# The last twelve batches of a per-batch adapter with residual and layer norm, in a written-out order

## The chip, the cores and the metric

The kernel runs on one core of a Trainium2 chip. The metric is the device time of one execution in microseconds. TensorE does matrix products into PSUM; VectorE, ScalarE and GpSimd do elementwise work; SyncE (SP) issues nearly all transfers between the chip's memory and SBUF. Each engine takes its instructions strictly in order, and they wait for each other through semaphores.

## The reference

For each of 128 batches `b` there is an `x[b]` of 128 rows and 512 columns and a language number `id`, which picks one of ten sets of weights. All is float32.

```python
h = relu(x @ W1[id] + b1[id])            # 512 -> 128, "down"
z = x + h @ W2[id] + b2[id]              # 128 -> 512, "up"; z is a residual sum
mean, var = mean(z), mean((z - mean)**2) # over the 512 columns
out = x + (z - mean) * rsqrt(var + 1e-5) * gamma[id] + beta[id]
```

## The kernel before, in words

One batch is one tile of 128 partitions by 512 columns. `B` is 128 and `E` is `B - 5`, which is 123. Each batch passes through the same steps; the name of the helper and its line stand behind each.

- TensorE transposes `x` in four blocks (`transpose_x`, L271), ScalarE copies the result to SBUF (`copy_xT`, L275).
- ScalarE copies the batch's W1 out of a table of all ten in SBUF, at an address that depends on the identifier (`stage_w1`, L262), into a tile of a pool of seven buffers. The first seventeen batches instead load W1 by identifier from the chip's memory (`load_first`, L161).
- TensorE multiplies (`down`, L294: four products in float32, each shown as two in the profile), ScalarE applies the bias and relu (`relu`, L302), TensorE multiplies by W2 (`up`, L311), into one of five PSUM buffers called `py`. The last two batches add b2 in TensorE as well, with a product that picks a row (L310).
- GpSimd makes `r = x + b2` (`add_b2`, L281) and `o = x + beta` (`add_beta`, L288).
- VectorE adds `r` to `py` and sums the rows in the same pass (`residual`, L328); ScalarE squares the deviations and sums them (`square`, L351).
- ScalarE makes the negative mean (L342) and a first estimate of the reciprocal root (`root`, L361); VectorE improves it with one Newton step, in three small instructions (L365, L367, L370). These small ones are done for two batches at once.
- VectorE scales, `py = (py - mean) * gamma` (`scale`, L394), and finishes, `o = py * rstd + o` (`finish`, L403).
- SP stores `o` for two batches at a time (`store`, L407), 512 KB each.

The order of the work is that of the program: `keep` chains each instruction behind the one before it on its engine. The main loop (L577) runs over `i`, and a step of it holds the transposes and the down product of one batch, the up product of an earlier one, and the normalisation of still earlier ones. TensorE's order in it is: transposes of `n`, down of `n - 1`, up of `n - 2`. At the end `tail` (L463) takes over for the batches behind `E`: there batches 123, 124 and 125 leave VectorE in the last step. ScalarE makes `n` (`by_pool`, L450), GpSimd multiplies by gamma for 123 and 124 (L452) and adds `o` (L454); 126 and 127 are finished by VectorE (`finish_cols`, L461), 127 in two halves. The last stores go out by batch or half a batch, on SP and on ScalarE's queue (`store_last`, L457).

Loads of `x` come four batches at a time, 1 MB each (`load_x`, L71); the last one is for batches 124 to 127.

Of the kernel before, what the change touches and what calls it, by code (L numbers as in the profile page):

```python
# [8 lines left out]
FP = mybir.dt.float32  # L9
# [7 lines left out]
P = 128  # L17
# [5 lines left out]
U = 2  # L23
# [3 lines left out]
def cond_resid_kernel(ctx: ExitStack, tc: tile.TileContext, x, itok, W1, b1, W2, b2, gamma, beta, out):  # L27
# [286 lines left out]
    def col(tiles, b):  # L314

        return tiles[b // 2][:, b % 2 : b % 2 + 1]
# [6 lines left out]
    def residual(b):  # L323
        r = rs.pop(b) if b in rs else xb(b)
        if b % 2 == 0:
            sums[b // 2] = st.tile([P, 2], FP, tag="sum", name=f"sum_{b // 2}")
        keep(
            nc.vector.scalar_tensor_tensor(ys[b], ys[b], 1.0, r, ALU.mult, ALU.add, accum_out=col(sums, b))  # L328
        )
# [30 lines left out]
    def root(ssq, t):  # L360
        keep(nc.scalar.activation(t, ssq, AF.Abs_reciprocal_sqrt, bias=eps, scale=1.0 / H3))  # L361

    def newton(n, ssq, t, u):
        if n == 1:
            keep(nc.vector.scalar_tensor_tensor(u, ssq, EPS * H3, t, ALU.add, ALU.mult))  # L365
        else:
            keep(nc.vector.scalar_tensor_tensor(u, u, 1.0 / H3, t, ALU.mult, ALU.mult))  # L367

    def newton_3(rstd, t, u):
        keep(nc.vector.scalar_tensor_tensor(rstd, u, -3.0, t, ALU.add, ALU.mult))  # L370
# [28 lines left out]
    def finish(b):  # L399
        g, j = divmod(b, 2)  # L400
        o = os[g][:, j, :]
        keep(
            nc.vector.scalar_tensor_tensor(o, ys.pop(b), rstds[g][:, j : j + 1], o, ALU.mult, ALU.add)  # L403
        )

    def store(g):
        keep(nc.sync.dma_start(out=out[2 * g : 2 * g + 2].rearrange("b s h -> s b h"), in_=os.pop(g)))  # L407
        del rstds[g]

    def on(b):  # L410
        return 0 <= b < B
# [3 lines left out]
    shifts = {}  # L415
    halves = slice(0, H // 2), slice(H // 2, H)

    def of_one(b):
        if -b not in parts_of:
            pool, tag = {E + 3: (p_h, "h"), E + 4: (p_x, "xT")}.get(b, (p_s, "s"))  # L420
            parts_of[-b] = pool.tile([P, 1], FP, tag=tag, name=f"root_of_{b}"), st.tile([P, 1], FP, tag="part", name=f"part_of_{b}")
        return parts_of[-b]

    def rstd_of(b, n):

        t, u = of_one(b)
        if n < 3:
            newton(n, ssqs[b], t, u)
        else:
            rstds[b] = st.tile([P, 1], FP, tag="rstd", name=f"rstd_{b}")  # L430
            newton_3(rstds[b], t, u)

    def deviation_of(b):
        ssqs[b] = st.tile([P, 1], FP, tag="ssq", name=f"ssq_{b}")
        sq = tp.tile([P, H], FP, tag="sq", name=f"sq_{b}")
        keep(nc.scalar.activation(sq, ys[b], AF.Square, bias=col(sums, b), scale=-float(H), accum_out=ssqs[b]))  # L436
        root(ssqs[b], of_one(b)[0])

    def rstd_col(b):
        return rstds[b] if b > E else rstds[b // 2][:, b % 2 : b % 2 + 1]  # L440

    def shift(b):
        shifts[b] = st.tile([P, 1], FP, tag="shift", name=f"shift_{b}")
        keep(nc.vector.tensor_scalar(shifts[b], col(nmeans, b), rstd_col(b), None, ALU.mult))

    def by_pool(b, scaled, cols=slice(0, H)):

        n = rp.tile([P, H], FP, tag="r", name=f"n_{b}")[:, cols]
        bias = 0.0 if scaled else shifts[b]
        keep(nc.scalar.activation(n, ys[b][:, cols], AF.Identity, bias=bias, scale=rstd_col(b)))  # L450
        if not scaled:
            keep(nc.gpsimd.tensor_tensor(n, n, gamma_b[:, bass.ds(lid(b, ET.Pool) * H, H)], ALU.mult))  # L452
        for part in halves if b > E else (cols,):
            keep(nc.gpsimd.tensor_tensor(os[b // 2][:, b % 2, part], n[:, part], os[b // 2][:, b % 2, part], ALU.add))  # L454
# [4 lines left out]
    def finish_cols(b, cols=slice(0, H)):  # L459
        o = os[b // 2][:, b % 2, cols]  # L460
        keep(nc.vector.scalar_tensor_tensor(o, ys[b][:, cols], rstd_col(b), o, ALU.mult, ALU.add))  # L461

    def tail(b):  # L463
        p = E // 2
        residual(b)
        if b == E + 1:
            rstd(p, 1)
            scale(E - 1)
            rstd(p, 2)
            finish(E - 2)  # L470
            store(p - 1)
            rstd(p, 3)
            deviation_of(b)
            shift(E)
            by_pool(E, False)
        elif b == E + 2:
            rstd_of(b - 1, 1)
            negative_means(b // 2)
            rstd_of(b - 1, 2)
            finish_cols(E - 1)  # L480
            store_last(E - 1)
            rstd_of(b - 1, 3)
            store_last(E)
            deviation_of(b)
        elif b == E + 3:
            left, right = slice(0, H // 2), slice(H // 2, H)
            few, most = slice(0, H // 4), slice(H // 4, H)
            shift(b - 2)
            by_pool(b - 2, False)
            residual(b + 1)  # L490
            rstd_of(b - 1, 1)
            scale(b - 1)
            rstd_of(b - 1, 2)
            deviation_of(b)
            negative_means(b // 2)
            scale(b)
            rstd_of(b - 1, 3)
            rstd_of(b, 1)
            deviation_of(b + 1)
            rstd_of(b, 2)  # L500
            by_pool(b - 1, True)
            for part in halves:
                store_last(b - 2, nc.scalar, part)
            for part in halves:
                store_last(b - 1, nc.scalar, part)
            rstd_of(b, 3)
            rstd_of(b + 1, 1)
            finish_cols(b)
            store_last(b)
            rstd_of(b + 1, 2)  # L510
            scale(b + 1)
            rstd_of(b + 1, 3)
            for cols in (left, right):
                finish_cols(b + 1, cols)
                store_last(b + 1, nc.sync, cols)


    def spin(n, width):
        idle = p_s.tile([P, H], FP, tag="s", name="idle")
# [54 lines left out]
    up(1)  # L574

    turned = 5
    for i in range(3, B + U):  # L577
        b = i - U - 1
        if b > G and b % G == 2 and b // G + 3 < NG and b // G + 3 >= 5:
            load_x(b // G + 3)  # L580
        up_to = i
        if b <= E:
            if turned <= up_to and on(turned):
                transpose_x(turned)
            add_b2(b + 2)
# [18 lines left out]
        if b == E:  # L604
            add_b2(b + 3)
            add_beta(b + 1)
            add_b2(b + 4)
            for n in range(b + 2, B):
                add_beta(n)
        if b > E:  # L610
            tail(b)
        elif half == 0:
            if on(b):
                vector_b2(b)
                residual(b)
                square(b)
            if mine:
                scale(2 * p)
                rstd(p, 1)
            if old:  # L620
                finish(2 * p - 1)
                store(p - 1)
        else:
            if on(b):
                vector_b2(b)
            if mine:
                rstd(p, 2)
            if on(b):
                residual(b)
                square(b)  # L630
            if mine:
                rstd(p, 3)
                scale(2 * p + 1)
            if mine:
                finish(2 * p)
        if 0 <= g and b <= E and half == 1:
            scalar_means(g)
            deviation(g)

        for n, engine in ((turned + 2, ET.Activation), (i - U + 3, ET.PE), (b + 1, ET.DVE), (b + 6, ET.Pool)):  # L640
            if on(n):
                lid(n, engine)


# [35 lines left out]
```

## Time and profile before

| what | value |
|---|---|
| time, median of 3 runs | 304.56 us (304.44 to 304.68) |
| the profiled execution's own time | 304.08 us |
| its span, first to last instruction | 302.3 us |
| granted TensorE clock, mean | 0.993 |
| busy: TensorE, VectorE, ScalarE, GpSimd | 96%, 97%, 92%, 94% |

Four engines are busy for over nine tenths of the span, so a batch has little slack on any of them. A busy share is not the same as a bound: in the stretch where TensorE sets the pace, VectorE's share is high because its instructions overlap in the record, each starting before the record of the one before has ended. The times below are microseconds from the start of the span. The stretch that matters here is the last one, from some 277 us on:

| stretch, us | VectorE | ScalarE | GpSimd | TensorE | GB/s |
|---|---|---|---|---|---|
| 270 to 280 | 9.96 | 9.82 | 10.00 | 10.00 | 171 |
| 280 to 290 | 9.72 | 9.82 | 10.00 | 10.00 | 116 |
| 290 to 299.2 | 8.78 | 6.16 | 8.22 | 3.47 | 165 |
| 299.2 to 302.3 | 0 | 0 | 0 | 0 | 187 |

The figures are the busy microseconds of each engine in the stretch.

### The profile page before, as it was taken

The page shows a single profiled execution, that of the slowest core. Times are in us where ns is not written, and L with a number is a line of the kernel's source. Part 1 is how long each engine was busy: PE and PEld are TensorE (multiplying, and loading weights), DVE is VectorE, ACT ScalarE, POOL GpSimd, SP SyncE. Part 2 cuts the span into 40 slices and gives each one's busy share as a digit, 9 for nine tenths or more (in the row PEclk, how much of TensorE's full clock was granted, in tenths as well). Part 3 has the DMA queues.
Part 4 walks back from the last instruction along what each step waited for, and adds up shares of the span by engine and source line. Part 5 has one row for each costly group of instructions (what it writes and reads, how often), then busy time and mean ns, then how long its engine had stood idle before and what let it go on. Part 6 is the DMA issues. An engine that isn't in the chain of part 4 may idle for free.

```text
span 302.3 us, 7001 instructions
## 1 busy us (share of the span) xinstructions
PE 290.6 (96%) x1820; PEld 218.0 (72%) x1821; DVE 294.2 (97%) x784; ACT 279.6 (92%) x771; POOL 284.9 (94%) x240
## 2 busy tenths in 40 slices
PE   7899999999999999999999999999999999999980
PEld 3758787777777777777777777777777777777740
DVE  6989999999999999999999999999999999999995
ACT  5878789999999999999999999999999999999982
POOL 1299998999999999999999999999999999999995
PEclk9999999999999999999999999999999999999997
DMA  6999999986667876766678667767866666882244
GB/s 235 385 389 364 346 339 402 404 307 206 233 234 243 279 255 205 244 209 261 222 280 270 212 204 240 263 226 261 279 211 221 218 253 217 271 283 113 108 166 173
DMA packets 43929, 77.33 MB, mean 256 GB/s; under 512 B 2121, under 2 KB 8020, under 8 KB 43890
## 3 DMA queue, kind: packets, MB, share of 16 engines
q1 hardware_dynamic: 43254, 76.31, 73.5%
q10 hardware_dynamic: 636, 0.57, 0.6%
q8 instruction: 15, 0.25, 0.3%
q14 instruction: 24, 0.20, 0.2%
HBM read 43.32 MB, written 33.55 MB: 254 GB/s over the span
## 4 chain that ended last, share of the span: by engine, by line
PE 89%; DVE 5%; DMA 2%; issue 1%; ACT 1%; SPq 0%; POOL 0%; DVEq 0%; ACTq 0%; POOLq 0%
PE ph L294 36%; PE py L311 35%; PE pxT L271 18%; DMA x<-in_x_dram 2%; DVE py L394 2%; DVE py L328 1%; DVE o L403 1%; PE row L229 1%; SPq L161 0%; ACT n L450 0%; ACT sq L351 0%; ACT sq L436 0%; DVE o L461 0%; ACT w1s L262 0%; DVE rstd L370 0%
## 5 line engine op out<-in xcount | busy, mean ns | idle before, releaser
L288 POOL TENSOR_TENSOR o<-x,beta_b 128x512 f32<-128x512 f32 x128 | 170.1, 1359 | 12.7 <-DVE beta_b L247 11.6
L294 PE MATMUL ph<-xT,w1s 128*128 128x128 f32 x1024 | 135.3, 275 | 0.2 <-DMA w1s<-in_L_cond_W_dram 0.2
L281 POOL TENSOR_TENSOR r<-x,b_b 128x512 f32<-128x512 f32 x97 | 131.7, 1360 | 0.0
L311 PE MATMUL py<-w,hT 128*128 x256 | 131.3, 595 | 0.0
L294 PEld LDWEIGHTS ph<-xT,w1s 128*128 128x128 f32 x1024 | 124.8, 192 | 1.3 <-issue 0.6
L271 PEld LDWEIGHTS pxT<-ident,x 128*128 128x128 f32 x512 | 66.0, 149 | 66.8 <-issue 49.9
L394 DVE SCALAR_TENSOR_TENSOR py<-py,nmean,gamma_b 128x512 f32<-128x512 f32 x126 | 94.8, 753 | 0.0
L403 DVE SCALAR_TENSOR_TENSOR o<-py,rstd,o 128x512 f32<-128x512 f32 x122 | 91.1, 747 | 0.0
L351 ACT ACTIVATE sq<-py,sum 128x512 f32<-128x512 f32 x124 | 85.8, 692 | 0.6 <-DVE py L328 0.6
L275 ACT COPY xT<-pxT 128x512 f32<-128x512 f32 x128 | 74.7, 583 | 4.3 <-PE pxT L271 4.1
L271 PE MATMUL pxT<-ident,x 128*128 128x128 f32 x512 | 77.6, 274 | 0.8 <-DMA x<-in_x_dram 0.6
L262 ACT COPY w1s<-w 128x512 f32 x111 | 68.0, 613 | 0.0
L328 DVE SCALAR_TENSOR_TENSOR py<-py,r 128x512 f32<-128x512 f32 x97 | 66.9, 690 | 0.2
L302 ACT ACTIVATE hT<-ph,b1T 128x128 f32<-128x128 f32 x128 | 46.9, 367 | 8.8 <-PE ph L294 4.2
L311 PEld LDWEIGHTS py<-w,hT 128*128 128x128 f32 x256 | 39.1, 192 | 1.4 <-issue 0.7
L351 ACT ACTIVATION_READ_ACCUMULATOR sq<-py,sum 128x1 f32 x124 | 25.1, 202 | 0.0
L328 DVE SCALAR_TENSOR_TENSOR py<-py,x 128x512 f32<-128x512 f32 x31 | 21.7, 699 | 1.4 <-PE py L311 1.1
L321 DVE TENSOR_TENSOR py<-py,b_b 128x512 f32<-128x512 f32 x27 | 18.6, 689 | 0.1
L361 ACT ACTIVATE root<-ssq,eps 128x2 f32<-128x2 f32 x62 | 16.5, 265 | 0.0
L328 DVE DVE_READ_ACCUMULATOR py<-py,r 128x1 f32 x97 | 13.6, 140 | 0.0
L342 ACT ACTIVATE nmean<-sum 128x2 f32<-128x2 f32 x62 | 12.3, 198 | 0.0
L365 DVE SCALAR_TENSOR_TENSOR part<-ssq,root 128x2 f32<-128x2 f32 x62 | 9.3, 149 | 0.2 <-ACT root L361 0.2
(57 smaller groups left out, 81.2 us busy)
## 6 DMA issues: line engine op xcount, KB each, us to landing
out_dram<-o SPq DMA_DIRECT2D x61, 512.0 KB, 3.3
x<-in_x_dram SPq DMA_DIRECT2D x27, 1024.0 KB, 6.7
x<-in_x_dram SPq DMA_DIRECT2D x10, 512.0 KB, 7.2
w1s<-in_L_cond_W_dram SPq DMA_DIRECT2D x17, 256.0 KB, 8.7
w<-in_L_cond_W_dram SPq DMA_DIRECT2D x4, 640.0 KB, 8.2
w<-in_L_cond_W_dram SPq DMA_DIRECT2D x1, 1792.0 KB, 9.8
w<-in_L_cond_W_dram SPq DMA_DIRECT2D x1, 768.0 KB, 5.3
out_dram<-o SPq DMA_DIRECT2D x3, 256.0 KB, 2.0
```

Of the source, the lines that this page charges most:

```text
L262: keep(nc.scalar.copy(w1s[b].rearrange("p k a -> p (k a)"), src))
L271: keep(nc.tensor.transpose(pxs[b][:, k, :], cols, ident))
L275: keep(nc.scalar.copy(xT[b], pxs.pop(b)))
L281: keep(nc.gpsimd.tensor_tensor(rs[b], xb(b), b2_b[:, bass.ds(v * H, H)], ALU.add))
L288: keep(nc.gpsimd.tensor_tensor(os[g][:, j, :], xb(b), beta_b[:, bass.ds(v * H, H)], ALU.add))
L294: nc.tensor.matmul(phs[b], lhsT=w1s[b][:, k, :], rhs=xT[b][:, k, :], start=(k == 0), stop=(k == KC - 1))
L302: keep(nc.scalar.activation(hT[b], phs.pop(b), AF.Relu, bias=b1T[:, bass.ds(lid(b, ET.Activation), 1)]))
L311: keep(nc.tensor.matmul(ys[b], lhsT=hT[b], rhs=w2[:, bass.ds(v * H, H)], start=not m, stop=True))
L328: nc.vector.scalar_tensor_tensor(ys[b], ys[b], 1.0, r, ALU.mult, ALU.add, accum_out=col(sums, b))
L351: nc.scalar.activation(sq, ys[b], AF.Square, bias=col(sums, b), scale=-float(H), accum_out=col(ssqs, b))
L394: nc.vector.scalar_tensor_tensor(ys[b], ys[b], col(nmeans, b), gamma_b[:, bass.ds(v * H, H)], ALU.add, ALU.mult)
L403: nc.vector.scalar_tensor_tensor(o, ys.pop(b), rstds[g][:, j : j + 1], o, ALU.mult, ALU.add)
```

## The change

The main loop ends six batches earlier (`range(3, B - 6)` instead of `range(3, B + U)`), and `tail` is gone. In its place stands a list of calls, one a step, for the rest: batches 116 to 127 in their last steps, 122 to 127 from the transposes on. All helpers keep to the order of that list on each engine. What differs in the work itself:

- Batch 125 is ended by TensorE. `base_of` makes `x + beta` in PSUM (a picked row and a product of the identity with `x`), VectorE's `scale_out` writes the scaled batch to SBUF, `diag_of` makes a diagonal matrix of its reciprocal deviations, `product_of` multiplies the two on top of the base, and ScalarE's `copy_out` moves the sum to `o`.
- Batches 119, 120, 123 and 124 are ended by ScalarE (`n_of`, scaled by rstd) and GpSimd (`add_of`); VectorE scales all of them. Before, 119 and 120 were ended by VectorE, and 123 and 124 had their gamma product on GpSimd.
- W1 of the last four batches is loaded by identifier from the chip's memory (`load_late`), in rows of 512 bytes, on SP's queue; ScalarE does not copy it.
- All stores are on SP's queue; ScalarE issues none.
- Means and roots of 124 to 127 are made one batch at a time.

```diff
-    for i in range(3, B + U):
+    for i in range(3, B - 6):
...
+    def n_of(b, scaled, cols=slice(0, H)):
+        rs[b] = rp.tile([P, H], FP, tag="r", name=f"n_{b}")
+        bias = 0.0 if scaled else shifts[b]
+        keep(nc.scalar.activation(rs[b][:, cols], ys[b][:, cols], AF.Identity, bias=bias, scale=rstd_col(b)))
...
+    def base_of(b, pool, tag):
+        base[b] = pool.tile([P, H], FP, tag=tag, name=f"base_{b}")
+        pick_b = pick[:, bass.ds(lid(b, ET.PE), 1)].to_broadcast([96, P])
+        keep(nc.tensor.matmul(base[b], lhsT=pick_b, rhs=parts[:96, :], start=True, stop=False))
+        keep(nc.tensor.matmul(base[b], lhsT=ident, rhs=xb(b), start=False, stop=True))
...
+            keep(nc.vector.tensor_scalar(diags[b], ident, rstd_col(b), None, ALU.mult))
+
+    def product_of(b, cols=slice(0, H)):
+        keep(nc.tensor.matmul(base[b][:, cols], lhsT=diags[b], rhs=rs[b][:, cols], start=False, stop=True, skip_group_check=True))
+
+    def copy_out(b, cols=slice(0, H)):
+        keep(nc.scalar.copy(out_of(b)[:, cols], base[b][:, cols]))
+
+    def load_late(b):
+        w1s[b] = wp.tile([P, KC, A], FP, tag="w1s", name=f"w1s_{b}")
+        src = W1[bass.ds(lid(b, ET.SP), 1)].rearrange("o (k p) a -> p (o k) a", k=KC)
+        keep(nc.sync.dma_start(out=w1s[b], in_=src))
...
+    lid(E + 1, ET.SP)
+    rstd(E // 2 - 3, 2)
+    load_late(E + 4)
+    residual(E - 4)
+    transpose_x(E - 1)
...
+    scale(E - 6)
+    load_late(E + 2)
+    load_late(E + 3)
+    transpose_x(E)
...
+    end_of(E - 7)
+    scale(E - 5)
...
+    scale(E - 4)
+    load_late(E + 1)
+    b2_of(E)
+    end_of(E - 6)
+    store_pair(E // 2 - 3)
...
+    transpose_x(E + 2)
+    residual(E - 1)
...
+    down(E + 1)
+    relu(E + 1)
+    up(E)
+    residual(E)
...
+    scale_out(E + 2)
+    store_pair(E // 2)
+    beta_of(E + 4)
+    root_of(E + 3)
+    rstd_of(E + 2, 3)
+    diag_of(E + 2, nc.vector)
+    n_of(E + 1, True)
+    add_of(E + 1, halves[1])
+    rstd_of(E + 3, 1)
+    base_of(E + 2, p_x, "xT")
+    residual(E + 4)
...
+    scale(E + 4)
+    store_last(E + 1, nc.sync, halves[0])
+    product_of(E + 2)
+    copy_out(E + 2)
+    store_last(E + 3, nc.sync)
+    store_last(E + 2, nc.sync)
+    rstd_of(E + 4, 2)
+    rstd_of(E + 4, 3)
+    end_of(E + 4, halves[1])
+    store_last(E + 4, nc.sync, halves[1])
+    end_of(E + 4, halves[0])
+    store_last(E + 4, nc.sync, halves[0])
```

More of the change, by code (lines that the diff above doesn't have):

```diff
@@ new lines, in mean_of, with add_of @@
+    def mean_of(b, engine):
+        if b // 2 not in nmeans:
+            nmeans[b // 2] = st.tile([P, 2], FP, tag="nmean", name=f"nmean_{b // 2}")
+        if engine is nc.scalar:
+            keep(nc.scalar.activation(col(nmeans, b), col(sums, b), AF.Copy, scale=-1.0 / H))
+        else:
+            keep(nc.vector.tensor_scalar(col(nmeans, b), col(sums, b), -1.0 / H, None, ALU.mult))
+    def add_of(b, cols=slice(0, H)):
+        o = out_of(b)[:, cols]
+        keep(nc.gpsimd.tensor_tensor(o, rs[b][:, cols], o, ALU.add))
@@ L424, in rstd_of, with square_of, root_of @@
+    def square_of(b):
+        ssqs[-b] = st.tile([P, 1], FP, tag="ssq", name=f"ssq_of_{b}")
+        sq = tp.tile([P, H], FP, tag="sq", name=f"sq_{b}")
+        keep(nc.scalar.activation(sq, ys[b], AF.Square, bias=col(sums, b), scale=-float(H), accum_out=ssqs[-b]))
+    def root_of(b):
+        parts_of[-b] = st.tile([P, 1], FP, tag="one", name=f"root_of_{b}"), st.tile([P, 1], FP, tag="part", name=f"part_of_{b}")
+        root(ssqs[-b], parts_of[-b][0])
     def rstd_of(b, n):
-        t, u = of_one(b)
+        t, u = parts_of[-b]
@@ L427, in rstd_of @@
         if n < 3:
-            newton(n, ssqs[b], t, u)
+            newton(n, ssqs[-b], t, u)
         else:
[L430 to L454, printed above, removed]
+            rstds[-b] = st.tile([P, 1], FP, tag="rstd", name=f"rstd_of_{b}")
@@ new lines, in scale_out, with diag_of @@
+    def scale_out(b):
+        v = lid(b, ET.DVE)
+        rs[b] = rp.tile([P, H], FP, tag="r", name=f"n_{b}")
+        keep(
+            nc.vector.scalar_tensor_tensor(
+                rs[b], ys[b], col(nmeans, b), gamma_b[:, bass.ds(v * H, H)], ALU.add, ALU.mult
+            )
+        )
+    diags = {}
+    def diag_of(b, engine):
+        diags[b] = st.tile([P, P], FP, tag="diag", name=f"diag_{b}", bufs=2)
+        if engine is nc.scalar:
+            keep(nc.scalar.activation(diags[b], ident, AF.Identity, scale=rstd_col(b)))
+        else:
+            keep(nc.vector.tensor_scalar(diags[b], ident, rstd_col(b), None, ALU.mult))
@@ L456, in store_last @@
     def store_last(b, engine=nc.sync, cols=slice(0, H)):
         keep(engine.dma_start(out=out[b][:, cols], in_=os[b // 2][:, b % 2, cols]))
[L459 to L515, printed above, removed]
@@ new lines, in cond_resid_kernel @@
+    end_of(E - 7)
+    scale(E - 5)
+    square(E - 4)
+    deviation(E // 2 - 2)
+    rstd(E // 2 - 2, 1)
+    down(E - 1)
+    residual(E - 3)
+    beta_of(E - 2)
+    rstd(E // 2 - 2, 2)
+    scale(E - 4)
[3 more added lines that the diff above has]
+    store_pair(E // 2 - 3)
+    stage_w1(E)
+    up(E - 2)
+    rstd(E // 2 - 2, 3)
+    beta_of(E + 3)
+    residual(E - 2)
+    copy_xT(E)
+    transpose_x(E + 1)
+    relu(E - 1)
+    down(E)
+    copy_xT(E + 1)
+    up(E - 1)
+    square(E - 3)
@@ new lines, in cond_resid_kernel @@
+    relu(E)
+    square(E - 2)
+    b2_of(E + 1)
+    deviation(E // 2 - 1)
+    end_of(E - 5)
+    negative_means(E // 2 - 1)
+    transpose_x(E + 2)
+    residual(E - 1)
+    scale(E - 3)
+    copy_xT(E + 2)
+    n_of(E - 4, True)
+    add_of(E - 4)
+    rstd(E // 2 - 1, 1)
+    beta_of(E + 1)
+    scale(E - 2)
+    rstd(E // 2 - 1, 2)
+    rstd(E // 2 - 1, 3)
+    down(E + 1)
+    relu(E + 1)
+    up(E)
+    residual(E)
+    square(E - 1)
+    transpose_x(E + 3)
+    copy_xT(E + 3)
+    end_of(E - 2)
@@ new lines, in cond_resid_kernel @@
+    scalar_means(E // 2)
+    scale(E - 1)
+    square(E)
+    scale(E)
+    beta_of(E)
+    down(E + 2)
+    relu(E + 2)
+    deviation(E // 2)
+    rstd(E // 2, 1)
+    n_of(E - 3, True)
+    rstd(E // 2, 2)
+    add_of(E - 3)
+    up(E + 1)
+    transpose_x(E + 4)
+    copy_xT(E + 4)
+    residual(E + 1)
+    down(E + 3)
+    rstd(E // 2, 3)
+    up(E + 2)
+    relu(E + 3)
+    up(E + 3)
+    mean_of(E + 1, nc.vector)
+    end_of(E - 1)
+    store_pair(E // 2 - 2)
+    residual(E + 2)
+    square_of(E + 1)
@@ new lines, in cond_resid_kernel @@
+    scale(E + 1)
+    n_of(E, True)
+    down(E + 4)
+    square_of(E + 2)
+    residual(E + 3)
+    root_of(E + 1)
+    rstd_of(E + 1, 1)
+    root_of(E + 2)
+    rstd_of(E + 2, 1)
+    relu(E + 4)
+    mean_of(E + 2, nc.vector)
+    square_of(E + 3)
+    mean_of(E + 3, nc.scalar)
+    store_pair(E // 2 - 1)
+    rstd_of(E + 1, 2)
+    add_of(E, halves[0])
+    up(E + 4)
+    rstd_of(E + 2, 2)
+    add_of(E, halves[1])
+    rstd_of(E + 1, 3)
+    scale_out(E + 2)
+    store_pair(E // 2)
+    beta_of(E + 4)
```

59 lines of the change are left out of this document (43 added, 16 removed).

## The prediction

> **What bounds the kernel now.** I read the page first, then the chain that ended last, then the windows and timelines of the last 25 us, where the two programs part. Busy shares from the page, then the chain from 274 us on (start, length, what):
>
> ```profile
> PE 290.6 (96%) x1820; PEld 218.0 (72%) x1821; DVE 294.2 (97%) x784; ACT 279.6 (92%) x771; POOL 284.9 (94%) x240
> ...
> 277.67 0.89 PE ph L294 x8
> 278.56 0.86 PE py L311 x2
> 279.42 0.45 PE pxT L271 x4
> 279.89 0.75 DVE py L328 x2
> ...
> 297.48 0.67 DVE py L394
> 298.15 0.07 DVE rstd L370
> 298.32 0.48 DVE o L461
> 298.81 0.39 DVEq L675
> ```
>
> Up to 279.9 the chain is TensorE alone: 0.44 transposes, 0.89 down, 0.86 up, 2.19 us a batch. Then it is VectorE to the end. How much room VectorE has in that stretch:
>
> ```profile
> 277.82:299.20 21.38, 20.68 (x65) 0.98 0.38 146
> ```
>
> ```profile
> 277.82 0.15 DVE L367 SCALAR_TENSOR_TENSOR part<-part,root 128x2 f32<-128x2 f32 x1
> 277.88 0.69 DVE L328 SCALAR_TENSOR_TENSOR py<-py,r 128x512 f32<-128x512 f32 x1
> 278.49 0.14 DVE L328 DVE_READ_ACCUMULATOR py<-py,r 128x1 f32 x1
> 278.49 0.15 DVE L370 SCALAR_TENSOR_TENSOR rstd<-part,root 128x2 f32<-128x2 f32 x1
> 278.56 0.75 DVE L394 SCALAR_TENSOR_TENSOR py<-py,nmean,gamma_b 128x512 f32<-128x512 f32 x1
> 279.22 0.75 DVE L403 SCALAR_TENSOR_TENSOR o<-py,rstd,o 128x512 f32<-128x512 f32 x1
> 279.89 0.69 DVE L328 SCALAR_TENSOR_TENSOR py<-py,r 128x512 f32<-128x512 f32 x1
> ...
> 296.04 0.15 DVE L365 SCALAR_TENSOR_TENSOR part_of<-ssq,root_of 128x1 f32<-128x1 f32 x1
> 296.22 0.16 DVE L367 SCALAR_TENSOR_TENSOR part_of<-part_of,root_of 128x1 f32<-128x1 f32 x1
> 296.41 0.15 DVE L370 SCALAR_TENSOR_TENSOR rstd<-part_of,root_of 128x1 f32<-128x1 f32 x1
> ...
> 298.32 0.88 DVE L461 SCALAR_TENSOR_TENSOR o<-py,rstd,o 128x256 f32<-128x256 f32 x2
> ```
>
> Busy times overlap, so steps are read from start to start: a wide instruction (scale, end) 0.67, a residual 0.61, a small one 0.065; a Newton step directly behind the one it reads starts 0.18 after it instead, 0.12 lost. The last two halves end at 299.20 and the span at 302.3: 3.1 us of store and closing.
>
> **The change, part by part.** The programs part at 277.8 on VectorE, at the first of the rows above, and on the other engines within about a microsecond of it. All before that stays.
>
> VectorE's list. Before and after it holds 17 wide instructions, 9 residuals, 23 Newton steps, four instructions for means or shifts, and the two halves of batch 127: what ScalarE and GpSimd take over (the ends of 119 and 120) is balanced by the scales of 123 and 124, which come back. New is only the diagonal. Work before: 17 x 0.67 + 9 x 0.61 + 23 x 0.065 + about 0.5 + 0.88 = 19.8 us of the 21.4, so 1.6 us idle, in waits for TensorE's products and between dependent small steps. The diagonal is not in the trace: between the one-column operation's 0.21 busy (shift row below) and the half-width row's 0.48, nearest the first by its single input tile; I take 0.25. In the new order I count seven places where a Newton step, the diagonal or an end stands right behind the step it reads, 0.12 each: with the mean of 124, read soon after, about 0.9 us of idle. If no other engine is late, VectorE ends 1.6 - 0.9 - 0.25 = 0.45 us sooner.
>
> ```profile
> L444 DVE TENSOR_SCALAR shift<-nmean,rstd 128x1 f32<-128x1 f32 x2 | 0.4, 210 | 0.0
> L262 ACT COPY w1s<-w 128x512 f32 x111 | 68.0, 613 | 0.0
> L281 POOL TENSOR_TENSOR r<-x,b_b 128x512 f32<-128x512 f32 x97 | 131.7, 1360 | 0.0
> ```
>
> ScalarE loses four W1 copies of 0.61 and gains one scaled pass and the copy out of 125, both like that copy: about 1 us less, off the path. GpSimd loses two gamma products and one beta sum and gains one add, 2.5 us less: its adds of 124 are covered by VectorE's last 3 us. TensorE gains the base of 125 (a row pick and an identity product) and the diagonal product, two products of 0.86 each as `up`; they stand behind the last `up`, so they cost only 125's own path. That path is base and product, some 2 us, and the copy, 0.6, then its store; from the last `up` VectorE still has residual, scale, end, scale, Newton steps and halves, about 4.3 us, so the copy has some 1.5 us of cover, after which 127's two stores would queue behind 125's on SP. I cost it at nothing.
>
> The W1 loads by identifier are the term that decides. They are four DMAs on SP's queue, in the order 127, 125, 126, 124, after one register load, and all stand behind the store of pair 57 (o of batches 114 and 115), which SP cannot issue before VectorE's end of 115. The first of them to be needed, 124, is the last to be issued. When they can start and when 124 is due:
>
> ```profile
> 277.93 0.37 SPq L407 DMA_DIRECT2D out_dram<-o  x1
> ...
> 33.08 0.76 SPq L103 DMA_DIRECT2D w<-in_L_cond_W_dram  x1
> 34.47 2.26 SPq L161 DMA_DIRECT2D w1s<-in_L_cond_W_dram  x1
> ...
> 284.08 1.06 PE L294 MATMUL ph<-xT,w1s 128*128 128x128 f32 x8
> ```
>
> The second pair has a register load between the two issues: 34.47 - 33.08 - 0.76 = 0.63. So the first W1 load issues at 277.93 + 0.37 + 0.63 = 278.9. The down product of 124 starts at 284.1 in the kernel before, and the new TensorE order leads to it with the same steps. What a megabyte of reading takes when it follows a 512 KB store 0.48 us later on the same queue (an x load): three late ones, issued at 238.8, 264.7 and 256.5, then the stages of pair 57's store in the kernel before, with nothing behind it, and of the second of these loads, whose store issues at 264.25:
>
> ```profile
> x<-in_x_dram SPq DMA_DIRECT2D x1, 1024.0 KB, 6.2
> ...
> x<-in_x_dram SPq DMA_DIRECT2D x1, 1024.0 KB, 7.0
> ...
> x<-in_x_dram SPq DMA_DIRECT2D x1, 1024.0 KB, 8.6
> ...
> 278.75:280.25 1.50, 1.50 (x11) 1.13 (x10) 1.50 (x3) 1.50 (x6) 1.50 (x2) 1.00 0.90 350
> 280.25:281.00 0.75, 0.75 (x6) 0.54 (x5) 0.75 (x3) 0.75 (x3) 0.75 (x2) 1.00 0.00 0
> ...
> 265.00:266.50 1.50, 1.50 (x10) 0.97 (x10) 1.50 (x5) 1.41 (x4) 1.50 (x2) 1.00 0.90 321
> 266.75:267.50 0.75, 0.75 (x9) 0.75 (x8) 0.75 (x4) 0.75 (x5) 0.75 (x2) 1.00 0.88 55
> 268.25:271.25 3.00, 3.00 (x22) 2.42 (x21) 3.00 (x9) 2.91 (x8) 3.00 (x4) 1.00 1.04 405
> ...
> 29.00:29.25 0.25, 0.25 (x5) 0.25 (x4) 0.25 (x2) 0.25 (x3) 0.25 (x2) 1.00 1.16 299
> ```
>
> The last column is GB/s. A store runs for 1.5 us; after the one at 264.25 comes most of a microsecond with little moving though the load has long been issued, then 405 GB/s. The four W1 loads are together the same 1.05 MB, but in rows of 512 bytes; the stage at 29 us, where W1's other loads of such rows run, moves 299 GB/s: 3.5 us instead of 2.6, 0.9 more. Counted from the store's issue, x lands after 6.2 + 0.48 = 6.7, 7.5 or 9.1 us; so 124's weights land at 277.93 + 0.9 + these = 285.5, 286.3 or 287.9. I take 286.0, between the first two, for four transfers may pass an occasional late DMA engine better than one. The bound from below is no wait at all (landed by 284.1).
>
> **The Trainium skill** (DMA: Bandwidth & Descriptors, Specifications) gives 512 bytes as the least size of transfer at which the line rate is reached. By that the W1 rows would move like x, 0.9 us sooner, at 285.1, and the time would be 304.9. The rows disagree, 299 against 405 GB/s, and I go by the rows.
>
> From there on TensorE waits in order: the product of 124 is followed by the up product of 123, which VectorE's residual of 123 needs. 286.0 + 0.1 + 0.89 + 0.86 + 0.2 for the product's end = 288.1. From residual 123 VectorE's list is dense: 5 residuals 3.05, nine wide 6.03, 15 small 0.98, two means 0.26, the diagonal 0.25, halves 0.88, dependent idle 0.9: 12.4 us. It ends at 300.5, against 299.20: 1.3 us later. The profiled execution took 304.08 (span 302.3, so 1.8 around it), hence 305.4 there; the median of the runs before is 304.56, 0.48 above the profiled one, hence **305.8 us**.
>
> **Rivals.**
> First, the weights come in time and VectorE alone decides: 304.08 - 0.45 + 0.48 = 304.1. It holds if the load lands by 284.3, 5.4 us after the first issue. For it: pair 57's store is through by 280.3, and no x load competes any more. Against it: no late x load landed in under 6.2 us, and these rows are slower.
> Second, the other side: with the weights in time, the new order also takes the rest of VectorE's idle, because ScalarE's results stand ready before the Newton steps: 1.6 - 0.25 = 1.35 us, 303.2. From 0.61 us of closed idle on (0.2% of 304.56) it is faster. Against it: the steps of 0.18 between dependent Newton instructions are VectorE's own.
> Third, the loads run at x's rate (405 GB/s): landing at 285.1, end 300.55 - 0.9 = 299.6, 304.9.
> Fourth, a late DMA engine as in the 8.6 us load: 287.9, end 302.4, 307.7.
> Fifth, 125's copy is late and its store holds 127's on SP: with 1.5 us of cover it costs nothing; each microsecond beyond adds one. Its inputs shift with the same wait, so I give it little.
>
> **How the numbers follow.** Weights late by over a microsecond (305.2 to 307.0): 0.63; a late engine beyond that: 0.05; 125's store: 0.02; loads at x's rate or a little slower: 0.10; in time with Newton waits as counted: 0.09; in time and the idle closed: 0.11. A change under 0.2% (0.61 us) cannot be told from none here. Slower than 305.17: 0.63 + 0.05 + 0.02 = 0.70; within: 0.10 + 0.09 = 0.19; faster: 0.11. Range: from 304.0, which leaves out the case of the closed idle, to 307.2, which leaves out most late engines.
>
> **What would show it.** TensorE's down product of 124 starts near 286 instead of 284.1, with W1's DMA named as its releaser, and VectorE has a gap of over a microsecond before residual 123; after that VectorE is dense. The issues of the four loads stand at 279 to 281 in SP's timeline. If TensorE shows no such wait and VectorE's last half ends near 298.7, the landing estimate is wrong and the first rival holds; if residual 127 waits for TensorE although 124 was on time, ScalarE's relu of 127 was late, a wait I have left out.

## The result and the profile after

The changed kernel took 308.04 us (median of 5 runs, 307.93 to 309.17), the kernel before 304.44 (304.35 to 304.68) beside it: a ratio of 1.0126, interval 1.0116 to 1.0137, slower by 3.6 us. The prediction said slower, at 305.8 us, with a range up to 307.2; the time lies 0.8 us above the range.

The profiled execution of the changed kernel took 309.17 us, with 1.5 us more than the kernel before spent at its start, ahead of anything that the change touches. So the two traces are compared from one row that both have, the issue of pair 57's store on SP: at 277.93 us before (shown above) and at 279.45 after. From there to the end of the span it is 302.3 - 277.93 = 24.4 us before and 307.3 - 279.45 = 27.9 after, 3.5 more. To put a time of after on the clock of before, take off 1.52.

The page of the changed kernel, its span and the busy times:

```profile
span 307.3 us, 7020 instructions
...
PE 296.1 (96%) x1826; PEld 220.8 (72%) x1826; DVE 296.3 (96%) x785; ACT 279.2 (91%) x769; POOL 282.6 (92%) x238
```

The shares say nothing of the 3.5 us, but the busy time of VectorE does say something: 296.3 us against 294.2 before, 2.1 more for one instruction more. The chain that ended last shows where (start, length, what):

```profile
277.90 0.86 PE py L311 x2
...
279.19 0.91 PE ph L294 x8
...
282.33 5.15 DMA w1s<-in_L_cond_W_dram
...
287.61 1.13 PE ph L294 x8
288.74 0.88 PE py L311 x2
...
290.99 1.41 DVE py L394 x2
...
296.49 1.16 DVE part_of L367 x2
```

Two things stand in it that the kernel before did not have: a load of W1, and a Newton step of VectorE (L367) of 1.16 us, where such steps took 0.15.

The load first. SP's queue, then TensorE, then VectorE at batch 123, from the timelines of the changed kernel (start, length; in brackets the idle time before it and what ended it):

```profile
279.45 0.37 SPq L407 DMA_DIRECT2D out_dram<-o  x1
280.43 2.30 SPq L505 DMA_DIRECT2D w1s<-in_L_cond_W_dram  x4
```

```profile
287.61 1.13 PE L294 MATMUL ph<-xT,w1s 128*128 128x128 f32 x8 [1.70 <-DMA w1s<-in_L_cond_W_dram]
```

```profile
289.71 0.70 DVE L328 SCALAR_TENSOR_TENSOR py<-py,r 128x512 f32<-128x512 f32 x1 [1.76 <-PE py L311]
```

The last of the four loads, that of batch 124, is issued at 282.33 and lands 5.15 later, at 287.48, or 285.96 on the clock of before. TensorE has waited 1.70 us for it, and VectorE 1.76 us for TensorE behind it.

Now VectorE and GpSimd between the last residuals, from the same timelines:

```profile
296.00 0.43 DVE L365 SCALAR_TENSOR_TENSOR part_of<-ssq_of,root_of 128x1 f32<-128x1 f32 x2
296.35 0.14 DVE L443 TENSOR_SCALAR nmean<-sum 128x1 f32<-128x1 f32 x1
296.41 1.24 DVE L367 SCALAR_TENSOR_TENSOR part_of<-part_of,root_of 128x1 f32<-128x1 f32 x2
297.62 0.16 DVE L370 SCALAR_TENSOR_TENSOR rstd_of<-part_of,root_of 128x1 f32<-128x1 f32 x1
297.74 0.75 DVE L482 SCALAR_TENSOR_TENSOR n<-py,nmean,gamma_b 128x512 f32<-128x512 f32 x1
298.41 0.15 DVE L370 SCALAR_TENSOR_TENSOR rstd_of<-part_of,root_of 128x1 f32<-128x1 f32 x1
298.60 0.78 DVE L494 TENSOR_SCALAR diag<-ident,rstd_of 128x128 f32<-128x128 f32 x1
299.30 0.70 DVE L365 SCALAR_TENSOR_TENSOR part_of<-ssq_of,root_of 128x1 f32<-128x1 f32 x1
...
303.29 0.88 DVE L476 SCALAR_TENSOR_TENSOR o<-py,rstd_of,o 128x256 f32<-128x256 f32 x2
```

```profile
294.92 1.42 POOL L447 TENSOR_TENSOR o<-n,o 128x256 f32<-128x256 f32 x2 [1.12 <-ACT n L435]
296.30 1.27 POOL L423 TENSOR_TENSOR o<-x,beta_b 128x512 f32<-128x512 f32 x1
298.57 1.41 POOL L447 TENSOR_TENSOR o<-n,o 128x256 f32<-128x256 f32 x2 [1.01 <-ACT n L435]
```

The reader is to lay the two side by side. The first L367 begins at 296.41 and ends at 297.58; GpSimd's L423 runs from 296.30 to 297.57. The L365 at 299.30 ends at 300.00; GpSimd's second half ends at 299.98. In the first row, the first of the two L365 alone takes 0.36 and ends at 296.36; GpSimd's halves end at 296.34. The diagonal ends at 299.38, just behind the first half of the last pair, which ends at 299.30. So four short instructions of VectorE, three Newton steps and the diagonal, last until an instruction of GpSimd is through. For all that time the record shows VectorE as busy, with no idle gap to catch the eye. The tile that the three Newton steps read, in both kernels, is `root_of`, the first root estimate of the last batches. Its view (shortest, median and longest duration in ns, first and last start), before and then after:

```profile
L365 DVE SCALAR_TENSOR_TENSOR part_of<-ssq,root_of x4: 148/148/151, 291.7 to 296.5; 128x1 f32<-128x1 f32 x4
L367 DVE SCALAR_TENSOR_TENSOR part_of<-part_of,root_of x4: 144/152/156, 291.9 to 297.3; 128x1 f32<-128x1 f32 x4
```

```profile
L365 DVE SCALAR_TENSOR_TENSOR part_of<-ssq_of,root_of x4: 147/254/696, 296.0 to 302.1; 128x1 f32<-128x1 f32 x4
L367 DVE SCALAR_TENSOR_TENSOR part_of<-part_of,root_of x4: 147/148/1169, 296.4 to 302.8; 128x1 f32<-128x1 f32 x4
```

No step takes over 156 ns before; after, the longest take 696 and 1169, while the steps behind GpSimd's last instruction take 0.15 us with the same operands. In between lies a line of the change that the core of the diff above leaves out, the one which says where the estimate lies:

```diff
-            pool, tag = {E + 3: (p_h, "h"), E + 4: (p_x, "xT")}.get(b, (p_s, "s"))
-            parts_of[-b] = pool.tile([P, 1], FP, tag=tag, name=f"root_of_{b}"), st.tile([P, 1], FP, tag="part", name=f"part_of_{b}")
...
+        parts_of[-b] = st.tile([P, 1], FP, tag="one", name=f"root_of_{b}"), st.tile([P, 1], FP, tag="part", name=f"part_of_{b}")
```

Before, ScalarE wrote the estimates of the last batches to PSUM (`p_s`, `p_h` and `p_x` are PSUM pools), so each Newton step read one tile from there. After, they lie in SBUF, and all that the step reads lies in SBUF.

The theory at this point, called P in the texts below: of the 3.5 us, the load costs what was predicted, and the rest is VectorE standing still behind GpSimd in steps that read SBUF alone. The rivals: the late load is all, and the long steps follow from it (called W below); the small steps are long by their operands alone, whatever GpSimd does; or the new order itself (other neighbours, the diagonal) costs the time.

### The profile page after: what moved, and what is told of

It is laid out like the page before. It is cut to its first block, busy times and chain, and to the rows that moved or that the text cites. A ratio compares the mean times of both kernels' runs of the same rounds, so it can differ in the third digit from the quotient of the medians.

```text
span 307.3 us, 7020 instructions
## 1 busy us (share of the span) xinstructions
PE 296.1 (96%) x1826; PEld 220.8 (72%) x1826; DVE 296.3 (96%) x785; ACT 279.2 (91%) x769; POOL 282.6 (92%) x238
## 4 chain that ended last, share of the span: by engine, by line
PE 90%; DVE 4%; DMA 2%; issue 1%; ACT 1%; ACTq 0%; DVEq 0%
PE ph L294 36%; PE py L311 34%; PE pxT L271 18%; DMA w1s<-in_L_cond_W_dram 2%; PE row L229 1%; DVE py L394 1%; DVE py L328 1%; DVE o L476 1%; DMA rows<-in_L_cond_b_dram 1%; DVE part_of L367 0%; DVE part_of L365 0%; PE idle L517 0%; DVE diag L494 0%; ACT sq L351 0%; DVE n L482 0%
## 5 line engine op out<-in xcount | busy, mean ns | idle before, releaser
L288 POOL TENSOR_TENSOR o<-x,beta_b 128x512 f32<-128x512 f32 x121 | 159.6, 1343 | 12.8 <-DVE beta_b L247 12.8
L281 POOL TENSOR_TENSOR r<-x,b_b 128x512 f32<-128x512 f32 x92 | 123.7, 1345 | 0.0
L403 DVE SCALAR_TENSOR_TENSOR o<-py,rstd,o 128x512 f32<-128x512 f32 x116 | 86.6, 747 | 0.0
L271 PE MATMUL pxT<-ident,x 128*128 128x128 f32 x512 | 78.4, 276 | 0.0
L262 ACT COPY w1s<-w 128x512 f32 x107 | 65.5, 612 | 0.0
L370 DVE SCALAR_TENSOR_TENSOR rstd<-part,root 128x2 f32<-128x2 f32 x62 | 9.3, 150 | 0.0
```

The source lines that it names most:

```text
L262: keep(nc.scalar.copy(w1s[b].rearrange("p k a -> p (k a)"), src))
L271: keep(nc.tensor.transpose(pxs[b][:, k, :], cols, ident))
L281: keep(nc.gpsimd.tensor_tensor(rs[b], xb(b), b2_b[:, bass.ds(v * H, H)], ALU.add))
L288: keep(nc.gpsimd.tensor_tensor(os[g][:, j, :], xb(b), beta_b[:, bass.ds(v * H, H)], ALU.add))
L403: nc.vector.scalar_tensor_tensor(o, ys[b], rstds[g][:, j : j + 1], o, ALU.mult, ALU.add)
```

## The experiments

The kernel before ran in 304.73, 304.48, 304.33 and 304.35 us (medians) beside the four groups of runs; each ratio is against its own. "From the fork" below counts from the end of VectorE's last instruction for batch 115 (277.90 us before, 279.43 after), up to which all the kernels do the same work on VectorE; the last half of 127 ends 21.30 us after it in the profile before and 24.74 in the one after.

**The roots in PSUM, first try.** One PSUM tile with four columns, a column for each batch:

```diff
-        parts_of[-b] = st.tile([P, 1], FP, tag="one", name=f"root_of_{b}"), st.tile([P, 1], FP, tag="part", name=f"part_of_{b}")
+        if 0 not in single:
+            single[0] = p_s.tile([P, 4], FP, tag="s", name="root_of")
+        parts_of[-b] = single[0][:, b - E - 1 : b - E], st.tile([P, 1], FP, tag="part", name=f"part_of_{b}")
```

> The first estimates of the reciprocal root of batches 124 to 127 lie in PSUM, in four columns of one tile, as the kernel before had them there; nothing else differs from the changed kernel. Theory P (a VectorE instruction whose inputs all lie in SBUF stands still while GpSimd works on SBUF): the Newton rows of 124 to 127 fall back to 0.15 us each, from 1.17, 0.70 and 0.36, though GpSimd runs as before; VectorE's list gets about 1.8 us shorter, 306.2 us. The diagonal keeps its 0.78. Theory W (W1's late landing is all, and the long rows follow from it): nothing moves, 308.0 us, and the long Newton rows stay.

307.40 us, ratio 1.0081 (1.0052 to 1.0110). The steps were short again (156 ns at most), the diagonal 285 ns, but the time fell by less than was expected: by 0.6 us by the medians, 1.4 by the ratios (0.0045 of 304.5). The profile has 1.83 from the fork, of which 0.66 is not the edit's: the product of 124 started 7.53 us after the fork, against 8.19 in the change. The fourth run shows what this edit brings in of its own.

**The loads in the order in which they are needed.** Only the order changes, 124, 125, 126, 127 instead of 127, 125, 126, 124; the roots stay in SBUF.

```diff
-    load_late(E + 4)
+    load_late(E + 1)
...
-    load_late(E + 1)
+    load_late(E + 4)
```

> The four W1 loads are issued in the order of need, 124, 125, 126, 127, at the same three places; nothing else differs from the changed kernel. Both theories: 124's weights land three quarters of a load set sooner, some 2.8 us, and TensorE's wait of 1.86 us ahead of the down product of 124 is gone. Theory P: the long Newton rows and the diagonal stay, though they may meet other GpSimd instructions; 1.3 us less than the changed kernel, 306.7 us, with 0.7 to either side for the meetings. Theory W: all of the 3.6 us goes, 304.4 us or less.

306.25 us, ratio 1.0051 (1.0034 to 1.0067): 1.8 us better than the change. TensorE no longer waits for a load: the down product of 124 starts 6.33 us after the fork, 6.18 before, 8.19 in the change. The held steps are still there, and at another place. VectorE and GpSimd in this run:

```profile
292.79 1.71 DVE L365 SCALAR_TENSOR_TENSOR part_of<-ssq_of,root_of 128x1 f32<-128x1 f32 x2
...
295.64 0.78 DVE L494 TENSOR_SCALAR diag<-ident,rstd_of 128x128 f32<-128x128 f32 x1
296.35 0.69 DVE L365 SCALAR_TENSOR_TENSOR part_of<-ssq_of,root_of 128x1 f32<-128x1 f32 x1
```

```profile
290.28 2.90 POOL L447 TENSOR_TENSOR o<-n,o 128x512 f32<-128x512 f32 x3
293.02 1.39 POOL L423 TENSOR_TENSOR o<-x,beta_b 128x512 f32<-128x512 f32 x1
```

The first of the two L365 here takes 1.64 us alone: it was held through the end of one GpSimd instruction (293.18) and all of the next, and ended at 294.44, when GpSimd was through at 294.41.

**The first try with the diagonal on ScalarE.**

```diff
-    diag_of(E + 2, nc.vector)
+    diag_of(E + 2, nc.scalar)
```

> As the run with the roots in PSUM, and the diagonal matrix of 125 is made by ScalarE instead of VectorE. Theory P: VectorE loses the 0.70 us step of the diagonal besides the Newton rows' 1.8; 2.3 to 2.5 us less than the changed kernel, 305.6 us. ScalarE gains some 0.3 us in a place where it waits. Theory W: 308.0 less the diagonal's own 0.2, 307.8 us.

306.47 us, ratio 1.0070 (1.0041 to 1.0100). Against the first try the last half came 0.17 us sooner from the fork, and the intervals overlap: little to tell, and a miss like the first.

**All three: one PSUM tile, the diagonal on ScalarE, the order of need.**

> Roots in PSUM, the diagonal by ScalarE, and W1 in the order of need. Theory P with W1's wait beside it: both causes gone, so what the prediction's first rival had, less the diagonal: VectorE ends 0.7 us sooner than in the kernel before, 303.8 us. If a third cause is left, the time stays above 304.4 us. Theory W: the same as the order of need alone.

304.79 us, ratio 1.0006 (0.9996 to 1.0015). Nothing is held and no load is late, yet the waits show what the first try had brought in itself (engine, tile and line, what for; us in total, times, longest):

```profile
DVE rstd_of L370 <- ACT root_of L361: 0.5, 1, 0.5
...
ACT root_of L361 <- DVE part_of L365: 0.4, 1, 0.4
DVE part_of L365 <- ACT root_of L361: 0.3, 1, 0.3
```

With four batches in columns of one tile, ScalarE's estimate for one batch waits for VectorE's step on another, and the other way round: 1.2 us in sum. The first and third runs have the same rows. The kernel before had spread the four over three places, and only 124 and 125 shared one.

**The roots in PSUM, each in a place of its own.** Nothing else is changed.

```diff
-        parts_of[-b] = st.tile([P, 1], FP, tag="one", name=f"root_of_{b}"), st.tile([P, 1], FP, tag="part", name=f"part_of_{b}")
+        pool, tag = {E + 2: (p_y, "y"), E + 3: (p_h, "h")}.get(b, (p_s, "s"))
+        parts_of[-b] = pool.tile([P, 1], FP, tag=tag, name=f"root_of_{b}"), st.tile([P, 1], FP, tag="part", name=f"part_of_{b}")
```

> As the changed kernel, the roots of 124 to 127 each in a PSUM place of its own (the pair roots' place, one of the five up-product places, relu's, the pair roots' again), so that none waits for another's reader as the four columns of one tile did (0.4 us of VectorE at batch 125, 0.5 at 126 in the run with all three edits). Theory P: all Newton rows at 0.15 us, no wait between the batches' roots; W1's wait of 1.2 to 1.9 us and the diagonal stay: 306.0 us, 2.0 less than the changed kernel. Theory W: 308.0 us.

305.05 us, ratio 1.0018 (1.0006 to 1.0029): 3.0 us better than the change by the medians, by the place of one small tile. The tile's view, two of the steps beside GpSimd, the product of 124, VectorE's residual behind it and its last halves:

```profile
L365 DVE SCALAR_TENSOR_TENSOR part_of<-ssq_of,root_of x4: 144/150/152, 294.4 to 298.2; 128x1 f32<-128x1 f32 x4
L367 DVE SCALAR_TENSOR_TENSOR part_of<-part_of,root_of x4: 148/149/152, 294.6 to 298.9; 128x1 f32<-128x1 f32 x4
```

```profile
294.57 0.21 DVE L367 SCALAR_TENSOR_TENSOR part_of<-part_of,root_of 128x1 f32<-128x1 f32 x2
294.76 0.15 DVE L370 SCALAR_TENSOR_TENSOR rstd_of<-part_of,root_of 128x1 f32<-128x1 f32 x1
```

```profile
294.67 1.27 POOL L423 TENSOR_TENSOR o<-x,beta_b 128x512 f32<-128x512 f32 x1
```

```profile
285.99 1.13 PE L294 MATMUL ph<-xT,w1s 128*128 128x128 f32 x8 [1.25 <-DMA w1s<-in_L_cond_W_dram]
```

```profile
288.08 0.70 DVE L328 SCALAR_TENSOR_TENSOR py<-py,r 128x512 f32<-128x512 f32 x1 [1.32 <-PE py L311]
...
299.38 0.88 DVE L477 SCALAR_TENSOR_TENSOR o<-py,rstd_of,o 128x256 f32<-128x256 f32 x2
```

From residual 123 to the end of the last half: 300.26 - 288.08 = 12.18 us here, 304.17 - 289.71 = 14.46 in the change. The difference, 2.28, is the sum of what the four held instructions took over their free length: L365 0.36 - 0.15, L367 1.17 - 0.15, diagonal 0.78 - 0.29, L365 0.70 - 0.15, together 2.27. The product of 124 also waited 0.45 us less for its load (1.25 against 1.70), which this edit does not explain.

**That, with the order of need and the diagonal on ScalarE.**

> As the run with all three edits, with the roots in places of their own. Theory P: VectorE's waits at 125's and 126's Newton steps (0.4 and 0.5 us) go; 304.0 us, 0.7 below the kernel before, whose first rival this is. If a third cause is left, 304.5 us or more.

303.78 us, ratio 0.9977 (0.9966 to 0.9987): faster than both kernels. VectorE's last half comes 20.52 us after the fork, and the waits of the first try are gone.

**The same, with W1 of the last four copied by ScalarE as before.** The four loads by identifier are taken out and `stage_w1` stands in their place, ahead of the products that need them.

```diff
-    load_late(E + 1)
...
+    stage_w1(E + 1)
```

> As the run before it in this list, but W1 of the last four is copied by ScalarE out of the table, as in the kernel before, instead of being loaded. Is the loading worth anything once it is in time? ScalarE has four copies of 0.51 us steps more in the stretch in which it follows TensorE. If ScalarE has room there, the same time as with the loads in order, 304.0 us; if it paces relu and the transposes' copies, up to 2 us more, 306.0 us.

304.51 us, ratio 0.9994 (0.9979 to 1.0008), 0.7 us more than with the loads. The down products of 126 and 127 start later, 11.30 and 14.28 us after the fork against 10.71 and 13.54. So the loads, when they come in time, are worth 0.7 us.

**The kernel before with its roots in SBUF.** The other way round, the one line of the change alone:

```diff
-            pool, tag = {E + 3: (p_h, "h"), E + 4: (p_x, "xT")}.get(b, (p_s, "s"))
-            parts_of[-b] = pool.tile([P, 1], FP, tag=tag, name=f"root_of_{b}"), st.tile([P, 1], FP, tag="part", name=f"part_of_{b}")
+            parts_of[-b] = st.tile([P, 1], FP, tag="one", name=f"root_of_{b}"), st.tile([P, 1], FP, tag="part", name=f"part_of_{b}")
```

> The kernel before, with the roots of 124 to 127 in SBUF as the change has them, and nothing else: one part of the change alone. Theory P: GpSimd works on SBUF from 292.1 to 298.8 us with few gaps, so several of the twelve Newton rows of 124 to 127 stretch to the end of the GpSimd instruction that runs (up to 1.2 us each); 1 to 3 us slower, 306.5 us. Theory W: no change, 304.6 us, rows at 0.15.

306.01 us, ratio 1.0043 (1.0024 to 1.0062): the line alone costs 1.5 us without any new order, diagonal or load. Its tile's view, and the longest L367 beside GpSimd, whose instruction ends at 297.03:

```profile
L367 DVE SCALAR_TENSOR_TENSOR part_of<-part_of,root_of x4: 152/268/961, 292.6 to 299.8; 128x1 f32<-128x1 f32 x4
L370 DVE SCALAR_TENSOR_TENSOR rstd<-part_of,root_of x4: 145/438/734, 293.4 to 300.7; 128x1 f32<-128x1 f32 x4
```

```profile
296.09 0.96 DVE L367 SCALAR_TENSOR_TENSOR part_of<-part_of,root_of 128x1 f32<-128x1 f32 x1
```

```profile
295.77 1.26 POOL L451 TENSOR_TENSOR n<-n,gamma_b 128x512 f32<-128x512 f32 x1 [0.36 <-ACT n L449]
```

**The diagonal back on VectorE**, in the fastest version:

> As the version with the roots in PSUM places of their own, the loads in order of need and the diagonal on ScalarE (303.78 us), but the diagonal is made by VectorE again, as in the changed kernel. If the diagonal is only its own work on VectorE (0.29 us where it stood free), 303.9 to 304.1 us. If it still is held by a GpSimd instruction, its row shows 0.5 to 0.8 us and the time is 304.2 to 304.6.

303.81 us, ratio 0.9978 (0.9969 to 0.9988). The diagonal took 288 ns and the last half came 0.09 us later from the fork; by the time it costs nothing that can be told. So the diagonal's own work is not the trouble; in the change it was held by what ran beside it.

**The loads in the change's order again**, in the fastest version:

> As the same version (303.78 us), but the W1 loads in the changed kernel's order, so that the one needed first is issued last. The down product of 124 then starts 1.4 us later, as in the run with the roots alone. By the theory that the wait passes to the end in full, less what VectorE had idle after it: 304.8 to 305.2 us. If the wait is hidden, 303.8.

305.43 us, ratio 1.0034 (1.0022 to 1.0045), 1.65 us more than in order of need, a little above what was expected. In its profile the product of 124 starts 1.35 us later and the last half comes 1.37 later: the wait passes to the end in full.

**The loads earlier**, in the fastest version: four of the main loop's steps before the list begins (the expectation says seven batches; it is four), in a pool of nine buffers.

```diff
+        if i == 118:
+            for n in range(E + 1, B):
+                load_late(n)
```

> As the same version (303.78 us), but the four W1 loads are issued seven batches of the main loop earlier, into a pool with two more buffers. The down product of 124 was on time already in that version, so by the theory nothing is won: 303.6 to 303.9 us. If the products of 125 to 127 still waited for their loads at a price, 303.2 to 303.5. If the loads hold up stores or the x load on SP's queue, 304 or more.

303.92 us, ratio 0.9985 (0.9975 to 0.9995): nothing won, as expected. In order of need the loads are early enough.

**GpSimd's x + beta of 127 earlier**, in the changed kernel, roots in SBUF:

```diff
     add_of(E - 3)
+    beta_of(E + 4)
...
     store_pair(E // 2)
-    beta_of(E + 4)
```

> The changed kernel as it is, roots in SBUF included, but GpSimd makes x + beta of batch 127 before the two half adds of batch 123, where GpSimd stood idle for 1.1 us, not behind them. Nothing is changed on VectorE. If VectorE's second Newton step of 124 took 1.17 us because GpSimd's x + beta of 127 was running, it takes 0.15 us now, VectorE is 0.8 to 1.0 us sooner, and the time is 307.0 to 307.3 us; the diagonal (0.78) and the step behind it (0.70) stay held by the half adds of 124. If the length belongs to the operands alone (SBUF slower to read, whatever GpSimd does), the row stays above 1 us and the time 308.0.

305.62 us, ratio 1.0034 (1.0017 to 1.0051): 2.4 us better by the medians, by moving one instruction of another engine into its idle time. In the profiles VectorE's list from residual 123 to the last half took 12.53 us against 14.46, 1.93 less. The tile's view, and GpSimd's rows:

```profile
L365 DVE SCALAR_TENSOR_TENSOR part_of<-ssq_of,root_of x4: 145/150/424, 295.0 to 299.2; 128x1 f32<-128x1 f32 x4
L367 DVE SCALAR_TENSOR_TENSOR part_of<-part_of,root_of x4: 143/148/236, 295.5 to 299.9; 128x1 f32<-128x1 f32 x4
```

```profile
292.75 1.27 POOL L423 TENSOR_TENSOR o<-x,beta_b 128x512 f32<-128x512 f32 x1
293.99 1.41 POOL L447 TENSOR_TENSOR o<-n,o 128x256 f32<-128x256 f32 x2
297.00 1.42 POOL L447 TENSOR_TENSOR o<-n,o 128x256 f32<-128x256 f32 x2 [1.60 <-ACT n L435]
```

The step of 1.17 us is gone with its operands unchanged, which rules out the rival of the slow operands. More came back than was expected: with 124's Newton steps through 1 us sooner behind residual 123, the half adds of 124 start only at 297.00, behind the diagonal (286 ns at 296.62) and the L365 at 296.82 (150 ns), so these two were free as well, which the expectation had left held.

Put as a table of medians, for the two causes:

| roots of 124 to 127 | loads 127, 125, 126, 124 | loads in order of need |
|---|---|---|
| in SBUF | 308.04 | 306.25 |
| in PSUM, own places | 305.05 | 303.81 |

The roots in SBUF cost 3.0 us with the loads in the change's order and 2.4 in order of need; the order costs 1.8 us with the roots in SBUF and 1.2 in PSUM. The four come from different groups of runs; by the ratios, each against its own kernel before, the roots cost 3.3 and 2.2 us and the order 2.3 and 1.2, so tenths are not to be read from the table.

The profiles give the sum for the changed kernel, from the fork to the end of the last half. Before, it is 21.30 us. The new order with both causes put right takes 20.62, 0.68 less. The change's order of loads adds 1.40 (22.01). The roots in SBUF add 2.73 (24.74): 2.28 in the held instructions, 0.45 in a longer wait for 124's load, which no run ties to the roots.

With both put right and nothing else touched (303.81), the change is 0.2% faster than the kernel before.

## Why the prediction was wrong

- **The W1 loads**, "the term that decides": right about the order, the queue and the lateness. 124's weights were to land at 286.0 and landed at 285.96 on the same clock. That it came so close is luck: counted from the issue of pair 57's store, the landing took 8.03 us here and 7.4 to 8.2 in the five other profiles with the same loads in the same order. The transfers ran below x's rate, as taken: a window of the changed kernel in which only W1 is on its way (the last column is GB/s) shows 285, against 299 in the row the estimate used, and 405 for x. One thing was left out: the store of pair 58 was issued at 284.32, and from 285.2 its data moved beside the last of the weights. What that cost was not tried. The third rival would have had 405. So would the rule of the Trainium skill (DMA: Bandwidth & Descriptors, Specifications) quoted there; the trace does not agree.

```profile
283.00:285.00 2.00, 2.00 (x15) 1.69 (x14) 2.00 (x6) 1.39 (x4) 2.00 (x2) 1.00 1.00 285
```

- **What waits behind the loads**: right. TensorE's product of 124 and VectorE's residual of 123 stood where they were said to. Residual 123 was to start at 288.1 and started at 289.71 - 1.52 = 288.19.
- **"From residual 123 VectorE's list is dense"**, with "15 small 0.98" and "the diagonal 0.25", 12.4 us in all: this is the step that failed. It took 14.46 us. The same list with the roots in PSUM took 12.18, so its count of work and of dependent idle was right to 0.2 us; the small steps and the diagonal were priced by rows that had an operand in PSUM or a single small input, and those of after had all of theirs in SBUF beside a busy GpSimd. In sum: 12.4, less 0.2 for that count, and 2.27 for what the four held instructions took over their free length, make the 14.46. With residual 123 0.1 us later than said, VectorE ended 2.15 us later than said, which is nearly all of the distance between 305.8 and 308.04, 2.24. The line that moves the roots stands in the diff and was passed over; none of the five rivals had it.
- **GpSimd "2.5 us less", costed at nothing**: GpSimd's busy time did fall, 284.9 to 282.6, but when it is busy came to count. That it is no bound does not make it free.
- **The first rival**, the weights in time, 304.1: its conditions were met in the runs with the order of need and PSUM roots, which took 303.81 with the diagonal on VectorE, 303.78 on ScalarE. VectorE's own account, 0.45 us sooner, is borne out and was if anything too low; in the profiles it was 0.68 and 0.78.
- **The second rival**, all of VectorE's idle closed, 303.2: no run came nearer than 303.78.
- **The fifth rival**, 125's copy and store: no cost. From the last half to the end of the span it is 3.15 us after and 3.13 before, as the "3.1 us of store and closing" had it.

## What to carry to other kernels

When a change moves a small tile between PSUM and SBUF, reprice every instruction that reads it: its length in the old trace holds only for the old place, and the engine to look at beside it is GpSimd. A load is to be issued in the order in which it is needed; here, against ScalarE's copies (304.51 us), the same four loads lost 0.9 us in one order (305.43) and won 0.7 in the other (303.78). An instruction of an engine that is no bound can still be moved to good effect, if it is moved out of the time of those it holds up. And a held instruction does not show as idle time: the sign of it is a row whose longest duration is far above the median (here 1169 against 148 ns).

## What the runs showed of the hardware

- A VectorE instruction on one column, 0.15 us by itself, took up to 1.17 us in the changed kernel and 1.64 in the run with the loads in order, when its operands all lay in SBUF and GpSimd was at work on SBUF operands. It ended within 0.1 us of the end of a GpSimd instruction in every row shown. With one operand in PSUM the same steps took 0.14 to 0.16 us beside the same GpSimd work.
- The Trainium skill has this (SBUF — State Buffer, Who interferes with whom): VectorE and GpSimd share a pair of ports, held for a whole instruction, and a VectorE instruction with two SBUF inputs contends with a GpSimd one that reads SBUF, while one with at most one SBUF input does not, unless it runs in a mode that takes both port pairs. The traces agree, for the three lines of the Newton step. The page also says that `tensor_scalar` can run in such a mode: the diagonal, 0.29 us free and 0.78 beside GpSimd's half adds, agrees. In two runs it began in the last 0.15 to 0.2 us of a GpSimd instruction and still took 0.29, so what is shown to hold it is a longer overlap than that.
- A `tensor_scalar` of one column (L443) was not held: 0.20 us at 294.62 in the kernel before with its roots in SBUF, inside a GpSimd instruction that ran from 294.15 to 295.41. Why the diagonal is and this is not was not tried.
- A held instruction need not get its turn when GpSimd's current instruction ends: the L365 of 1.64 us stayed through the end of one and all of the next, while the L365 of 0.36 us in the change came in between two. What decides that stays open.
- The wait of 124's product for its load was 1.70 us in the change and 1.03, 1.04, 1.25, 1.2 and 1.89 in the five other profiles with the same loads in the same order. The cause of this spread stays open; it may be behind part of the 3.0 against 2.4 us in the table.
